# Matrix square root and spectral layer on one core: earlier loads for the inverse transform, a schedule of three rounds in ten, filler matmuls, and a reordered start

## The chip, the cores and the metric

One core of a Trainium2 chip. The metric is device time in microseconds (us) of one execution. The kernel before took 3040.89 us, the median of three runs (3040.22 to 3058.99); lower is better. Engines are called TensorE (PE), VectorE (DVE), ScalarE (ACT), GpSimd (POOL) and SyncE (SP). PEld is TensorE's weight load.

## The reference, cut to what matters

The input x is (32 images, 32 channels, 128, 128) in float32. Each layer normalises x in 16 groups of two channels, transforms it, and adds the result to x.

```python
def _L0_conv_ref(A):                    # layer 0: matrix square root of every 128 x 128 channel
    normA = jnp.sqrt(jnp.sum(A2 * A2, axis=(1, 2)))
    Y = A2 / normA[:, None, None]; Z = I
    for _ in range(5):
        T = 0.5 * (3.0 * I - jnp.matmul(Z, Y)); Y = jnp.matmul(Y, T); Z = jnp.matmul(T, Z)
    return Y * jnp.sqrt(normA)[:, None, None]

def _L1_conv_ref(x, weights1, weights2): # layer 1: mixing of channels on low frequencies
    x_dht = fftn(x).real
    top = einsum('bixy,ioxy->boxy', x_dht[:, :, :32, :32], weights1)
    bot = einsum('bixy,ioxy->boxy', x_dht[:, :, -32:, :32], weights2)
    return ifftn(out_dht).real           # out_dht: zeros, with top and bot put in

x = x + _L0_conv_ref(_gn(x))
x = x + _L1_conv_ref(_gn(x), weights1, weights2)
```

## The kernel before

**Layer 0.** The work unit is a quartet: four channels of an image, 256 in all. prep (line 208) computes an image's statistics and scales: it loads eight tiles xs (two groups each) through ScalarE's DMA queue, in four buffers, three ahead; VectorE takes bn_stats of each; two small matmuls average over partitions; two square roots (root, line 171: a Sqrt on ScalarE and four operations of VectorE) give sc, the scale, and sn, the last factor. After the second root comes off, the offset that ScalarE needs to scale the rows. Only then does made[b] exist, and staged (356) may scale a quartet: POOL makes x from xt, ScalarE makes b. newton (426) then runs the iteration as some twenty steps. In a step TensorE makes four 128x128 products into a PSUM bank (products, 327; a float32 product is two records in the trace), and VectorE or ScalarE takes the bank. POOL adds r = mb + EYE (plus_eye, 313). The last step adds the root to xt (452). settle (458) stores it to the DRAM tensor mid, POOL folds it (halves added and subtracted), and VectorE takes its statistics.

**Layer 1.** After the eighth quartet of an image, forward (476), summed (511) and spectrum (544) compute its low frequencies from the folds. Images come in groups of 20, 7, 3 and 2 (GROUPS). When a group's spectra are there, wide_products, small_products (661) or last_products (740) multiply them with the weights, piece by piece of the frequencies; om holds a result on the chip, and od in DRAM collects it. small_products begins with two memsets on POOL and sixteen or more loads diag<-xs on SP. For the last group, weights() (782) loads the weights into buffers of layer 0 as these come free. Then inverse (887) takes each image: load_products reads ob (for small groups or, which place copies into order as ob), load_input (832) reads mid back as yt in two halves of channels (e = 0, 1; two tiles of 512 KB each). TensorE transforms the rows (pg, copied by ScalarE as gt) and then the columns (py). For each half e and each tile i, ScalarE copies the odd part as d, VectorE adds the even part to yt, and unfold (857) adds or subtracts d, on POOL (in the tail every other tile on VectorE). store (849) writes yt to the output. The pool page (three buffers) serves om, or and d; yt has six buffers, and in the tail some yt take buffers of fold.

**The order of the work.** Every engine and DMA queue works in the order in which the Python code issues instructions; that order is written by hand, with generators. The main loop (1042) runs rounds. In a round it steps each of nine lanes once, each lane being one quartet's newton. A new quartet starts every 3 rounds for images 1 to 18 and every 5 rounds for the others. Between the lanes it steps the other queues once: preps (1070), specs, posts, prods (the products), and backs (the inverse). prods is stepped in two of three rounds, backs in the third, and backs in the next round too when an inverse stands in the middle of a half (holding). Each yield in inverse is the end of such a turn. With the first yield (893), the one after pg (914) and two for each half, an image inside a group takes four turns, 12 rounds. When no quartet is left, tail is true, all these queues are stepped for every lane, and the stores go to ScalarE's DMA queue instead of SP's. From image 20 on, inverse, products and the last quartets run beside each other.

**Queues.** SP's queue carries mid, turn, the weights, od, ob or or, yt and, before the tail, the output. A DMA on it that waits (for a buffer, or for POOL's result) holds everything behind it. ScalarE's queue carries x, xt and xs, in line with ScalarE's own operations.

Of the kernel before, what the change touches and what calls it, by code (L numbers as in the profile page):

```python
# [36 lines left out]
P = 128  # L37
# [51 lines left out]
def conv_preact_kernel(  # L89
# [78 lines left out]
    def bank():  # L168
        return ps8.tile([P, 4, P], F32, tag="ps", name="ps")

    def root(v, n, tag):

        s0 = small.tile([P, n], F32, tag="root_0", name=f"{tag}_s0")
        nc.scalar.activation(s0, v, AF.Sqrt)
        yield
        q = small.tile([P, n], F32, tag="root_1", name=f"{tag}_q")
        nc.vector.reciprocal(q, s0)
        nc.vector.tensor_mul(q, q, v)
        nc.vector.tensor_tensor(q, q, s0, ALU.add)
        s = small.tile([P, n], F32, tag=f"{tag}_s", name=f"{tag}_s", bufs=3 if tag == "a_t" else 2)  # L180
        nc.vector.tensor_scalar_mul(s, q, 0.5)
        return s

    def moments(st, ms, tag):

# [22 lines left out]
    def prep(bs, made):  # L208

        n = len(bs)  # L210
        nc_, ng = n * C, n * G
        first_b = bs[0]
        st = small.tile([P, ng, 6], F32, tag="a_st", name=f"a_st{first_b}", bufs=2)
        tiles = []
        parts = [(b, i) for b in bs for i in range(C // 4)]

        def load(k):
            b, i = parts[k]
            t = stp.tile([P, 2, 2 * P], F32, tag="xs", name=f"xs{b}_{i}")
            src = xs_in[b, :, 2 * i : 2 * i + 2].rearrange("p g h c -> p g (h c)")  # L220
            kept(nc.scalar.dma_start(out=t, in_=src))
            tiles.append(t)

        for k in range(3):
            load(k)
        yield
        for k in range(len(parts)):
            for j in range(2):
                nc.vector.bn_stats(st[:, 2 * k + j, :], tiles[k][:, j, :])
            yield  # L230
            if k + 3 < len(parts):
                load(k + 3)
        ms = small.tile([P, ng], F32, tag="a_ms", name=f"a_ms{first_b}")
        nm, d = yield from moments(st, ms, "a")
        yield from pause
        pq = bank()[:, 0, 0:nc_]
        nc.tensor.matmul(pq, avg_mean, d.rearrange("p g c -> p (g c)"), start=True, stop=True)

        v = small.tile([P, nc_ + ng], F32, tag="a_v", name=f"a_v{first_b}")
        nc.vector.tensor_scalar_mul(v[:, 0:nc_], pq, -512 / (P * P))  # L240
        yield
        vg = small.tile([P, ng], F32, tag="a_vg", name=f"a_vg{first_b}")
        nc.vector.tensor_reduce(
            vg, v[:, 0:nc_].rearrange("p (g c) -> p g c", c=2), AX.X, ALU.add
        )
        nc.vector.tensor_scalar(v[:, nc_:], vg, 0.5, EPS, ALU.mult, ALU.add)
        yield
        s = yield from root(v, nc_ + ng, "a_r")
        iv = small.tile([P, nc_ + ng], F32, tag="a_inv", name=f"a_inv{first_b}")
        nc.vector.reciprocal(iv, s)  # L250
        yield

        sc = small.tile([P, nc_], F32, tag="a_sc", name=f"a_sc{first_b}", bufs=2)
        nc.vector.tensor_scalar_mul(sc, iv[:, 0:nc_], MS / P)
        nn = small.tile([P, ng, 2], F32, tag="a_d", name=f"a_n{first_b}")
        nc.vector.tensor_tensor(
            nn,
            s[:, 0:nc_].rearrange("p (g c) -> p g c", c=2),
            iv[:, nc_:, None].to_broadcast([P, ng, 2]),
            ALU.mult,  # L260
        )
        nn = nn.rearrange("p g c -> p (g c)")
        nc.vector.tensor_scalar_mul(nn, nn, P * (1.5 / (EYE * QF)) ** 2)
        yield
        sn = yield from root(nn, nc_, "a_t")

        off = small.tile([P, ng, 2], F32, tag="a_off", name=f"a_off{first_b}", bufs=2)
        nc.vector.tensor_tensor(
            off,
            sc.rearrange("p (g c) -> p g c", c=2),  # L270
            nm[:, :, None].to_broadcast([P, ng, 2]),
            ALU.mult,
        )
        off = off.rearrange("p g c -> p (g c)")
        for k, b in enumerate(bs):
            g, c = slice(k * G, k * G + G), slice(k * C, k * C + C)
            made[b] = (nm[:, g], sc[:, c], off[:, c], sn[:, c])
        yield


# [145 lines left out]
    def newton(g, sn, xt, m, mb, far, more):  # L426


        q = yield from quartic(m, mb, far, more, False)
        my = four("my", more)  # L430
        y = my[:, :, 0, :]
        nc.scalar.mul(y, products(q, m), 1 / (MS * QF))
        yield from rest
        m = my[:, :, 1, :]
        nc.scalar.mul(m, products(q, y), MS / QF)
        yield from rest
        mb = taken(transposed(m), "mb", more)
# [12 lines left out]
        t = plus(products(w, q), -0.5 * EYE / (1.5 * QF), eye, "t", more)  # L450
        yield from rest
        nc.vector.tensor_tensor(xt, products(t, y), xt, ALU.add)
        yield

    folds = {}
# [88 lines left out]
    def spectrum(b, u):  # L544
# [40 lines left out]
        if i == len(xs):  # L585

            for e, t in enumerate(diags):
                for l4 in range(4):
                    rows = slice(32 * l4, 32 * l4 + 32)
                    copy = nc.scalar.copy if l4 % 2 else nc.vector.tensor_copy  # L590
                    copy(
                        t.rearrange("p (m b l f) -> p m b l f", b=2, l=4, f=4)[rows, :, j, l4, :],
                        spec[rows, 8 * e : 8 * e + 8].rearrange("p k q (h f) -> p (k q h) f", f=4),
                    )
            yield
            return
        kept(
# [142 lines left out]
    def last_products(i):  # L740
# [4 lines left out]
        for kk in range(KK):  # L745
# [25 lines left out]
            if kk % 4 == 3:  # L771
                for f in range(4):
                    queue = nc.scalar if f % 2 else nc.sync
                    kept(
                        queue.dma_start(
                            out=od[i][f, kk - 3 : kk + 1].rearrange("k r x -> r k x"),
                            in_=om[f::4, :, f, :].rearrange("p (k h) o -> p k (h o)", h=2),
                        )
                    )
        yield  # L780

    def weights():
# [104 lines left out]
    def inverse(b):  # L887


        more = where[b][1] < GROUPS[where[b][0]] - 1  # L890
        load_products(b)
        load_input(b, 0)
        yield
        if b not in placed:
            place(b)
            if not tail:
                yield
# [12 lines left out]
        for e in range(2):  # L910
            gts.append(inv.tile([P, 4, P], F32, tag="gt", name=f"gt{b}_{e}", bufs=3))
            nc.scalar.copy(gts[e], pg[e])
        unfold()
        yield
        for e in range(2):
# [16 lines left out]
            for i in range(2):  # L932
# [11 lines left out]
                if not i:  # L944
                    holding.append(b)
                    yield
                    holding.pop()
            if not e:
                load_input(b, 1)
            elif more:  # L950
                load_input(b + 1, 0)
                place(b + 1)
            yield
        if not more:
            unfold()
# [79 lines left out]
            yield  # L1035

    preps.append(prep([0], made))
    coming = [((0, 0), [1])] + [((b - 2, 4 if b < FIRST else 2), [b, b + 1]) for b in range(2, B, 2)]
    fetch(*fetches.pop(0))
    stage()  # L1040
    fetch(*fetches.pop(0))
    while todo or any(lanes) or posts or specs or prods or backs:
# [3 lines left out]
        for i in range(LANES):  # L1046
# [26 lines left out]
                step(specs)  # L1073
            if i == 3 or tail:
                step(posts)
            if i == 0 and rounds % 3 or tail:
                step(prods)
            if i == 0 and (rounds % 3 == 0 or holding) or tail and not (posts or specs):
                step(backs)
        rounds += 1  # L1080

# [68 lines left out]
```

## Time and profile before

| | |
|---|---|
| median of three runs | 3040.89 us |
| the profiled execution | 3037.9 us, its span 3035.8 us |
| granted TensorE clock, mean | 0.983 |
| busy: PE | 2878.3 us (95%), 27076 records |
| busy: PE weight load | 2675.2 us (88%) |
| busy: DVE | 2263.7 us (75%) |
| busy: ACT | 1644.0 us (54%) |
| busy: POOL | 1987.6 us (65%) |
| DMA | 636.39 MB, mean 210 GB/s |

The span is the time from the first to the last instruction. The times in the text below are microseconds from its start. All instructions are recorded at line 83, a helper that keeps them in the order of the program, so groups are told apart by the names of their tiles: ps is a PSUM bank, and out<-in gives the tile written and those read. A row of the timeline is: start, busy time, engine, operation, tiles, forms, count, and in brackets how long the engine had been idle before and what ended that. Rows with SPq or ACTq are DMAs issued by that engine's queue; their duration is the time over which the issues spread, waits between them included. For several instructions in one row, the duration is the sum of busy time on an engine.

### The profile page before, as it was taken

The page shows a single profiled execution, that of the slowest core. Times are in us where ns is not written, and L with a number is a line of the kernel's source. Part 1 is how long each engine was busy: PE and PEld are TensorE (multiplying, and loading weights), DVE is VectorE, ACT ScalarE, POOL GpSimd, SP SyncE. Part 2 cuts the span into 40 slices and gives each one's busy share as a digit, 9 for nine tenths or more (in the row PEclk, how much of TensorE's full clock was granted, in tenths as well). Part 3 has the DMA queues.
Part 4 walks back from the last instruction along what each step waited for, and adds up shares of the span by engine and source line. Part 5 has one row for each costly group of instructions (what it writes and reads, how often), then busy time and mean ns, then how long its engine had stood idle before and what let it go on. Part 6 is the DMA issues. An engine that isn't in the chain of part 4 may idle for free. (4 is left out here: it accounts for less than half of the span.)

```text
span 3035.8 us, 73213 instructions
## 1 busy us (share of the span) xinstructions
PE 2878.3 (95%) x27076; PEld 2675.2 (88%) x27076; DVE 2263.7 (75%) x4261; ACT 1644.0 (54%) x4187; POOL 1987.6 (65%) x2306
## 2 busy tenths in 40 slices
PE   6999999999999999999999999999999999898973
PEld 6899999999999999999999889889888889797863
DVE  6778787878787888778876656877778767776654
ACT  3566565665656665565644445555555555564442
POOL 4577677777777776767765435678777774675542
PEclk9999999999999999999999999999999999999986
DMA  5576676777675768575733567667667677575585
GB/s 173 163 231 206 213 215 214 215 214 222 201 232 189 240 190 247 182 240 185 246 109 105 169 205 233 234 215 254 235 205 258 230 249 241 178 233 179 183 265 187
DMA packets 476658, 636.39 MB, mean 210 GB/s; under 512 B 97040, under 2 KB 257296, under 8 KB 476304
## 3 DMA queue, kind: packets, MB, share of 16 engines
q1 hardware_dynamic: 362400, 422.21, 43.3%
q10 hardware_dynamic: 113904, 209.50, 22.3%
q8 instruction: 217, 3.56, 0.5%
q14 instruction: 137, 1.12, 0.1%
HBM read 402.42 MB, written 229.11 MB: 208 GB/s over the span
## 5 line engine op out<-in xcount | busy, mean ns | idle before, releaser
L83 PE MATMUL ps<-my,q 128*128 128x128 f32 (+1 forms) x4096 | 736.4, 329 | 12.7 <-DVE v L83 9.8
L83 PEld LDWEIGHTS ps<-my,q 128*128 128x128 f32 x4096 | 625.8, 191 | 71.5 <-DVE v L83 11.4
L83 POOL TENSOR_TENSOR w<-w,r 128x512 f32<-128x512 f32 x288 | 366.7, 1275 | 379.2 <-DMA w<-turn 308.7
L83 PE MATMUL ps<-w,v 128*128 128x128 f32 x4096 | 552.5, 278 | 25.1 <-DVE w L83 12.4
L83 ACT ACTIVATE b<-b,a_off,a_sc 128x128 f32<-128x128 f32 x1024 | 469.8, 492 | 173.1 <-issue 47.5
L83 POOL TENSOR_TENSOR fold<-xt 128x256 f32<-128x256 f32 x512 | 363.3, 731 | 285.0 <-DVE xt L83 256.2
L83 PEld LDWEIGHTS ps<-w,v 128*128 128x128 f32 x4096 | 503.2, 193 | 40.0 <-DVE w L83 11.8
L83 ACT ACTIVATE my<-ps 128x512 f32<-128x512 f32 x512 | 306.1, 604 | 351.1 <-PE ps L83 333.7
L83 DVE SCALAR_TENSOR_TENSOR q<-ps,eye 128x512 f32<-128x512 f32 x512 | 350.4, 685 | 180.6 <-PE ps L83 175.8
L83 POOL TENSOR_TENSOR yt<-yt,d 128x512 f32<-128x512 f32 x242 | 304.3, 1280 | 273.1 <-ACT d L83 240.7
L83 ACT ACTIVATE t<-ps 128x256 f32<-128x256 f32 x512 | 191.2, 382 | 356.6 <-PE ps L83 345.7
L83 POOL TENSOR_TENSOR r<-mb,eye 128x512 f32<-128x512 f32 x256 | 326.3, 1275 | 79.1 <-ACT mb L83 79.1
L83 POOL TENSOR_SCALAR x<-xt,a_nm,a_sc 128x128 f32<-128x128 f32 x736 | 321.6, 450 | 21.3 <-DVE a_n L83 18.7
L83 POOL TENSOR_TENSOR r<-b,eye 128x512 f32<-128x512 f32 x256 | 326.5, 1275 | 2.7 <-ACT b L83 2.7
L83 ACT ACTIVATE y<-ps,a_t_s 128x128 f32<-128x128 f32 x1024 | 291.2, 375 | 0.0
L83 PE MATMUL ps<-x,b 128*128 128x128 f32 x2048 | 274.9, 278 | 7.5 <-POOL x L83 5.7
L83 PE MATMUL ps<-x,q 128*128 128x128 f32 x2048 | 274.4, 277 | 4.0 <-DVE q L83 2.2
L83 PE MATMUL ps<-y,t 128*128 128x128 f32 x2048 | 273.8, 277 | 2.3 <-DVE t L83 2.3
L83 PE MATMUL ps<-my,mb 128*128 128x128 f32 x2048 | 273.6, 277 | 0.4 <-DVE q L83 0.4
L83 PE MATMUL ps<-q,t 128*128 128x128 f32 x2048 | 274.1, 277 | 0.0
L83 DVE STREAM_TRANSPOSE turn<-v 128x512 f32<-128x512 f32 x288 | 264.9, 920 | 9.9
L83 PEld LDWEIGHTS ps<-x,b 128*128 128x128 f32 x2048 | 251.3, 193 | 11.0 <-POOL x L83 6.0
(121 smaller groups left out, 4481.1 us busy)
## 6 DMA issues: line engine op xcount, KB each, us to landing
turn<-turn SPq DMA_DIRECT2D x288, 256.0 KB
b<-in_x ACTq DMA_DIRECT2D x256, 256.0 KB
xt<-in_xt ACTq DMA_DIRECT2D x256, 256.0 KB
xs<-in_xs ACTq DMA_DIRECT2D x256, 256.0 KB
mid<-xt SPq DMA_DIRECT2D x256, 256.0 KB
yt<-mid SPq DMA_DIRECT2D x128, 512.0 KB
out<-yt SPq DMA_DIRECT2D x113, 512.0 KB
w<-turn SPq DMA_DIRECT2D x144, 256.0 KB
```

The lines of the kernel that those rows point to most:

```text
L83: return self.tc.keep_in_program_order(issue(*args, **kw))
```

## The change

Five edits:

- **Start.** The first image's prep issues all eight xs loads at once (four tiles from the pool xs, four from early buffers of the tile turn), and the main program steps it once ahead of the loads of the first quartet. The offset off and made[b] come ahead of the second root, whose result sn is a tile made early and filled later; root writes into a tile that it is given.
- **inverse.** An image whose ob is already placed no longer has the first turn (load, yield). The load of the second half of yt stands right behind the copies gt, a turn and a half sooner, with a store ahead of it; another store stands behind the turn in the middle of a half. In the tail, load_products and place of the next image come one image sooner.
- **Rounds.** backs is stepped in rounds 0, 3 and 7 of ten, prods in the other seven.
- **warm.** A new function issues matmuls of 512 columns that nothing reads: five in the first image's prep, two after the last quartet's last product, two after the last spectrum, nine after the last products. They lie on TensorE's queue and take a PSUM bank.
- **Names** of the tiles in root.

```diff
+    def warm(n):
+        ps = bank()
+        for _ in range(n):
+            nc.tensor.matmul(ps, ident, tab[:, 0:512], start=True, stop=True)
...
-    def root(v, n, tag):
+    def root(v, n, s):
...
+        ahead = 3 if first_b else 8
         def load(k):
             b, i = parts[k]
-            t = stp.tile([P, 2, 2 * P], F32, tag="xs", name=f"xs{b}_{i}")
+            if first_b or i < 4:
+                t = stp.tile([P, 2, 2 * P], F32, tag="xs", name=f"xs{b}_{i}")
+            else:
+                t = four("turn", True).rearrange("p (j c) x -> p j (c x)", j=2)
...
-        for k in range(3):
+        for k in range(ahead):
             load(k)
...
-            if k + 3 < len(parts):
-                load(k + 3)
+            if k + ahead < len(parts):
+                load(k + ahead)
...
         nc.tensor.matmul(pq, avg_mean, d.rearrange("p g c -> p (g c)"), start=True, stop=True)
+        if not first_b:
+            warm(5)
...
         nc.vector.tensor_scalar_mul(sc, iv[:, 0:nc_], MS / P)
+        off = small.tile([P, ng, 2], F32, tag="a_off", name=f"a_off{first_b}", bufs=2)
+        nc.vector.tensor_tensor(off, ...)
...
+        sn = small.tile([P, nc_], F32, tag="a_t_s", name=f"a_t_s{first_b}", bufs=3)
+        for k, b in enumerate(bs):
...
+            made[b] = (nm[:, g], sc[:, c], off[:, c], sn[:, c])
+        yield
...
-        sn = yield from root(nn, nc_, "a_t")
...
+        yield from root(nn, nc_, sn)
         yield
...
         nc.vector.tensor_tensor(xt, products(t, y), xt, ALU.add)
+        if not todo and lanes.count(None) == LANES - 1:
+            warm(2)
         yield
...
+            if tail:
+                warm(2)
             yield
             return
...
+        warm(9)
         yield
...
     def inverse(b):
         more = where[b][1] < GROUPS[where[b][0]] - 1
-        load_products(b)
-        load_input(b, 0)
-        yield
         if b not in placed:
+            load_products(b)
+            if tail and more:
+                load_products(b + 1)
+            load_input(b, 0)
+            yield
             place(b)
...
             nc.scalar.copy(gts[e], pg[e])
+        if tail and more:
+            place(b + 1)
+        store()
+        load_input(b, 1)
         unfold()
         yield
...
                     yield
                     holding.pop()
-            if not e:
-                load_input(b, 1)
-            elif more:
+                    store()
+            if e and more:
                 load_input(b + 1, 0)
-                place(b + 1)
+                if b + 1 not in placed:
+                    place(b + 1)
             yield
...
     preps.append(prep([0], made))
+    step(preps)
...
-            if i == 0 and rounds % 3 or tail:
+            turn = rounds % 10 in (0, 3, 7)
+            if i == 0 and not turn or tail:
                 step(prods)
-            if i == 0 and (rounds % 3 == 0 or holding) or tail and not (posts or specs):
+            if i == 0 and (turn or holding) or tail and not (posts or specs):
                 step(backs)
```

More of the change, by code (lines that the diff above doesn't have):

```diff
@@ L169, in bank @@
         return ps8.tile([P, 4, P], F32, tag="ps", name="ps")
-    def root(v, n, tag):
-        s0 = small.tile([P, n], F32, tag="root_0", name=f"{tag}_s0")
+    def warm(n):
[3 more added lines that the diff above has]
+    def root(v, n, s):
+        s0 = small.tile([P, n], F32, tag="root_0", name="root_0")
         nc.scalar.activation(s0, v, AF.Sqrt)
         yield
-        q = small.tile([P, n], F32, tag="root_1", name=f"{tag}_q")
+        q = small.tile([P, n], F32, tag="root_1", name="root_1")
         nc.vector.reciprocal(q, s0)
@@ L179, in root @@
         nc.vector.tensor_tensor(q, q, s0, ALU.add)
-        s = small.tile([P, n], F32, tag=f"{tag}_s", name=f"{tag}_s", bufs=3 if tag == "a_t" else 2)
         nc.vector.tensor_scalar_mul(s, q, 0.5)
-        return s
     def moments(st, ms, tag):
@@ L247, in prep @@
         yield
-        s = yield from root(v, nc_ + ng, "a_r")
+        s = small.tile([P, nc_ + ng], F32, tag="a_r_s", name=f"a_r_s{first_b}", bufs=2)
+        yield from root(v, nc_ + ng, s)
         iv = small.tile([P, nc_ + ng], F32, tag="a_inv", name=f"a_inv{first_b}")
@@ L254, in prep @@
         nc.vector.tensor_scalar_mul(sc, iv[:, 0:nc_], MS / P)
+        off = small.tile([P, ng, 2], F32, tag="a_off", name=f"a_off{first_b}", bufs=2)
+        nc.vector.tensor_tensor(
+            off,
+            sc.rearrange("p (g c) -> p g c", c=2),
+            nm[:, :, None].to_broadcast([P, ng, 2]),
+            ALU.mult,
+        )
+        off = off.rearrange("p g c -> p (g c)")
+        sn = small.tile([P, nc_], F32, tag="a_t_s", name=f"a_t_s{first_b}", bufs=3)
+        for k, b in enumerate(bs):
+            g, c = slice(k * G, k * G + G), slice(k * C, k * C + C)
+            made[b] = (nm[:, g], sc[:, c], off[:, c], sn[:, c])
+        yield
         nn = small.tile([P, ng, 2], F32, tag="a_d", name=f"a_n{first_b}")
@@ L264, in prep @@
         yield
-        sn = yield from root(nn, nc_, "a_t")
[L267 to L277, printed above, removed]
+        yield from root(nn, nc_, sn)
         yield
```

## The prediction, made before the changed kernel was run

> **What bounds the kernel now.** First the page, part 2 (busy tenths in 40 slices of 75.9 us; PEclk is the granted TensorE clock).
>
> ```profile
> PE   6999999999999999999999999999999999898973
> ...
> PEclk9999999999999999999999999999999999999986
> ```
>
> TensorE is full from the second slice to about the 37th, so only the first slice, the last three and dips between can give time. Busy time by stretch (columns: stretch, length, then busy us of PE, PE weight load, DVE, ACT, POOL, then clock, DMA share, GB/s) sizes them:
>
> ```profile
> 1000.00:1500.00 500.00, 494.39 (x4129) 467.06 (x4128) 413.30 (x775) 299.31 (x777) 357.76 (x396) 1.00 0.71 218
> ...
> 2750.00:2800.00 50.00, 37.69 (x397) 33.35 (x396) 30.41 (x49) 22.48 (x54) 32.40 (x36) 0.95 0.55 174
> ...
> 2940.00:2960.00 20.00, 2.62 (x23) 1.23 (x24) 5.68 (x15) 2.62 (x3) 5.80 (x6) 0.54 0.85 288
> ...
> 2980.00:3000.00 20.00, 3.39 (x16) 2.38 (x16) 7.71 (x11) 3.12 (x8) 5.48 (x4) 0.57 0.67 207
> ```
>
> In a full stretch PE is busy 494 of 500 us. The hole at 2750 has 12 us without PE; the stretches from 2940 to 3036 have 31.8 us of PE work in 96 us, at a clock of 0.54 to 0.77. Three timelines (start, busy us, engine, operation, idle before and what ended it) show why. The start:
>
> ```profile
> 1.66 8.88 ACTq L83 DMA_DIRECT2D xs<-in_xs  x8
> ...
> 7.46 2.71 DVE L83 BATCH_NORM_STATS2 a_st<-xs 128x6 f32<-128x256 f32 x8 [5.74 <-DMA xs<-in_xs]
> ...
> 22.12 0.49 ACT L83 ACTIVATE b<-b,a_off,a_sc 128x128 f32<-128x128 f32 x1 [1.62 <-DVE a_off L83]
> ...
> 22.71 2.05 PE L83 MATMUL ps<-x,b 128*128 128x128 f32 x8 [5.67 <-POOL x L83]
> ...
> 29.06 0.75 DVE L83 BATCH_NORM_STATS2 a_st<-xs 128x6 f32<-128x256 f32 x2 [3.57 <-DMA xs<-in_xs]
> ```
>
> ScalarE's queue issues the first image's eight loads over 8.9 us, because four buffers hold them; statistics end at 14.55 (13.14 + 1.41), TensorE's first real product is at 22.71, when the first scaled row of b is ready, and at 29.06 VectorE stands 3.57 us on the second image's load. The hole:
>
> ```profile
> 2799.80 1.29 DVE L83 TENSOR_TENSOR yt<-ps,yt 128x512 f32<-128x512 f32 x2 [11.55 <-DMA yt<-mid]
> ...
> 2801.74 3.69 PE L83 MATMUL ps<-my,q 128*128 128x256 f32 x8 [9.83 <-DVE v L83]
> ```
>
> VectorE waits 11.55 us for the second half of image 26's rows (yt<-mid); v stands behind it, and TensorE behind v. That load was issued only at 2791.59, behind sixteen diag<-xs loads (2777.74, 9.70 us on SP). The tail:
>
> ```profile
> 2941.16 5.83 SPq L83 DMA_DIRECT2D yt<-mid  x2
> ...
> 2950.03 1.29 DVE L83 TENSOR_TENSOR yt<-ps,yt 128x512 f32<-128x512 f32 x2 [11.72 <-DMA yt<-mid]
> ...
> 2951.24 0.68 DVE L83 TENSOR_TENSOR xt<-ps,xt 128x512 f32<-128x512 f32 x1
> ...
> 2952.97 27.77 SPq L83 DMA_DIRECT2D yt<-mid  x4
> ...
> 2980.85 9.06 SPq L83 DMA_DIRECT2D od<-om  x6
> ...
> 2987.93 0.69 DVE L83 COPY om<-ps 128x512 f32<-128x512 f32 x1 [12.94 <-DMA od<-om]
> ```
>
> VectorE waits 11.72 us for yt of image 28; the last xt stands behind it, though its product was finished at 2939.5. Later SP stands up to 27.77 us in yt loads that wait for buffers, the od stores stand behind them, and the om copies wait 12.94 us for the page that these stores read. Then the last two images:
>
> ```profile
> 3004.12 2.08 PE L83 MATMUL ps<-tab,ob 64*128 64x128 f32 x16 [12.18 <-ACT ob L83]
> ...
> 3018.94 0.59 ACT L83 COPY gt<-ps 128x512 f32<-128x512 f32 x1 [3.05 <-PE ps L83]
> ```
>
> **What the Trainium skill says.** "TensorE: Matmul & The Clock Gate", Part 1 (The HAM clock gate): the clock halves after an idle window of about 3.4 us and comes back after one busy window. The trace agrees: eight records of w,v take 2.08 us at 30.46 and 1.06 at 2887.72. The same part: VectorE and ScalarE are strict FIFO. The trace agrees: xt at 2951.24 stood behind yt. "Trainium Kernel Development and Optimization", Key Constraints: SP's and ACT's DMAs share the same 16 engines. From 2920 to 2940 they are 0.96 busy at 308 GB/s, so a load that is issued sooner there isn't sooner by as much. "SBUF — State Buffer", Who interferes with whom: a VectorE operation with two SBUF inputs waits for a GpSimd one that reads SBUF. The trace agrees: a 128x96 a_r_q product took 1.29 us at 2198.70 beside a yt pair on POOL, against 0.21 for 128x48 at 18.73.
>
> **The change, part by part**, against the execution's own span of 3035.8 (its time 3037.9; median of the runs 3040.89, so 5.1 is added to the span's sum).
>
> *Start.* All eight xs loads go out ahead of b and xt. The table and xs are 2.39 MB; 1.85 MB came from about 2.7 to 9.3 (280 GB/s), so the last lands at about 11, plus 0.7 for its statistics: 11.6 against 14.55, -3.0. The chain to a_sc keeps its 5.1 us: 19.86 becomes 16.9. The offset stands right behind it instead of behind a square root and four operations (21.87): another -2.0. So the first product could start at 17.7 instead of 22.71. But five warm products stand ahead of it in PE's queue, from 14.0. One is 512 columns, as much as one group of four 128-column products (eight records, 0.89 us a group in the tail, 1.7 to 2.1 cold): two to four cold and the rest warm are 6.0 to 7.7 us, ending 20.0 to 21.7. The first group then takes 1.06 instead of 2.05 and ends at 21.1 to 22.8 against 24.76: -2.0 to -3.7. Second image's statistics come a few rounds later, as the rest of the root is now stepped first: VectorE's stand before 29.73 (w had its inputs at 27.3) can go, 0 to -2.4. I take **-4.5**, bounds -2 and -6. After that PE is full, so it lasts.
>
> *Rows sooner, three rounds in ten.* Operations are the same in number; stores and loads on SP change place. An image now takes three turns instead of four: 10 rounds against 12. I counted rounds in the order of the programs: the last inverse of group 0 ends in round 820 instead of 858, of image 26 in 960 instead of 972, and small_products of the third group starts in 962 in both. So the sixteen diag<-xs loads no longer stand ahead of image 26's rows: -9.8 of PE wait, -1.8 for a cold group (3.69 against 1.89), +1.5 for a diag<-xs wait that stays and now has less beside it: **-10**. Against it, denser inverse work: on POOL 46 of the r additions stood right behind yt sums before, 40 now, but of x and fold right behind two of them 5 become 21. I take this at nothing, since PE has at most 6 us in 100 free here and others' work covers it; if that cover is gone, up to +10; if fewer r waits (56 us on VectorE in all) win, -6.
>
> *Tail, up to the first om.* Image 28 is three rounds ahead, and its second half is loaded ahead of mb, v and w weights: issued at about 2930 instead of 2941. The SP queue was given about 7.25 MB from 2921 to 2941 at some 320 GB/s, so I let it land near 2939 to 2940, where VectorE needs it at 2936: a stand of 2 to 3 us instead of 11.72. The stall goes to POOL: yt27_24's pair (2.5 us) now stands ahead of the last lane's r (+2.2), and yt28_24's pair, done by VectorE before, ahead of the last fold. Adding POOL's queue from 2922 in its new order (1.27 an operation, folds 1.4) ends the fold at 2946.4, against 2955.72: **-9.3**. From there to the first om copy are 13.1 us, 7.3 of them PE at half clock; the two pairs of warm products can halve a part: **-2** (bounds -3.5 and +1.3, if a cold pair, 3.4 us, holds up the first product).
>
> *The om wait.* By the addresses of the tiles yt30_24 takes yt28_24's buffer, and om3_8 still takes om3_0's page. That yt28 store stands on ACT right behind the first od pair now, not behind the second: from om to its landing 8.0 us instead of 11.1; then SP issues one yt load instead of two ahead of od, 0.5 MB less. om3_0 to om3_8 is 13.4 us instead of 19.1: **-5.7** (bounds -2 and -8). From om3_8 to the or loads I take 0: om3_12 now stands behind one more unfolding, +1, but 1 MB of yt29 ahead of od is gone, up to -3.
>
> *Last two images.* Nine warm products (8 us, up to 11) lie in the 14 us of od's way to memory and back: at nothing, +2 if they start late. With them -1 for each first group and pg, **-2**. ob31 is copied before image 30's yt, so pg31 is hidden; gt31 still stands on ACT behind two stores of image 30: 3018.94 becomes 3015.7, **-3**.
>
> Tail: -9.3 - 2 - 5.7 - 2 - 3 = **-22**. Sum -4.5 - 10 - 22 = -36.5: span 2999.3, about **3004** on the scale of the median.
>
> **Rivals.** B, the hole only moves: the PE wait of 2750 is replaced by another (21 x or fold additions behind two pairs; denser ACT and VectorE work). For it: PE has small gaps from 1900 to 2700 wherever yt runs; against: what stood there was one SP queue, which is empty of diag loads now. Mid 0 to +2: 3014 to 3016. C, the tail stays gated: the 16 DMA engines are full at 2920 to 2950, yt28_24 lands at 2945 or the buffer of yt30 again holds od. For it: share 0.96 and 0.85; against: the v, w and mb weights (1.5 MB) now stand behind it. Tail only -8 to -10: 3016 to 3018. D, the other side: not faster, because POOL becomes the bound of the near stage. Place: r behind two unfoldings, w on VectorE behind r, TensorE behind w, as at 2203.01, where PE stood 3.78 us. Price: one more pair, 2.5 us, in each of the 27 images of groups 0 and 1: +67, so 3071. It decides from 36.5/27 = 1.35 us an image. Against: POOL is at 65%, and r's directly behind pairs got fewer. E, the tail gains more: od lands as soon as it is issued and the clock stays whole, -10 more: 2992. That the change does nothing is excluded for the start and image 26 by the order of the queues.
>
> **How the numbers follow.** Forecast 0.52 (own range 2993 to 3012), B 0.20, C 0.16, D 0.06, E 0.06. One per cent is 30.4 us, 3010.5, about what a measurement of this kernel can tell from no change. Below it are E and most of the forecast's own range (0.46 of 0.52), and 0.04 of B and C: 0.56 faster. Slower by over 1% is the upper part of D, 0.05; within, 0.39. The range 2990 to 3026 takes in forecast, B, C and half of E, with the bound of denser work on B.
>
> **What would show it.** Right: first x,b product near 21 and eight records in about 1.1 us; no yt<-mid wait above 4 us on VectorE; image 26 finished before diag<-xs; last xt near 2942 less the 14 saved before; the om wait below 9 us; PEclk above 0.8 in the last slices. Wrong: PE waits behind r or x of over 3 us from 1900 to 2700 that sum to more than before (steps B, D); a long yt wait on SP ahead of od (C); a first product that waits for warm ones beyond 23.

## The result, and the profile after

The changed kernel took 3009.16 us, the median of four runs (3001.22 to 3015.01), against 3045.48 before on the same chip: ratio 0.9872, 95% interval 0.9829 to 0.9915. Measured again later (six runs) it was 3006.2 against 3043.57: 0.9878, 0.9854 to 0.9902. The forecast was 3004, range 2990 to 3026. The profiled execution took 3011.95 us with a span of 3010.2 (before 3037.9 and 3035.8). The spans differ by 25.6 us, the medians by 36 to 37: the profiled execution of before lies 3 to 11 us below the medians that before had in the later measurements (3041.16 to 3048.71).

The page, part 2, after (busy tenths of PE and granted clock, 40 slices):

```profile
PE   8899999999999999999999999999999999999995
...
PEclk9999999999999999999999999999999999999997
```

The last six slices read 999995 instead of 898973, the first 8 instead of 6, and the clock ends in 97 instead of 86. Fillers count as busy here: PE is busy for 2899.0 us in all instead of 2878.3, and fillers are 22.1 us of it. But the kernel without any fillers (below) also ends in 999994. Busy time by stretch, columns as before (stretch, length, busy us of PE, PE weight load, DVE, ACT, POOL, then clock, DMA share, GB/s):

```profile
1000.00:1500.00 500.00, 492.73 (x4114) 465.51 (x4113) 407.46 (x773) 298.81 (x774) 357.68 (x396) 1.00 0.70 217
2750.00:2800.00 50.00, 48.37 (x533) 43.91 (x532) 37.71 (x63) 25.20 (x63) 36.02 (x43) 1.00 0.54 185
2940.00:2960.00 20.00, 17.43 (x227) 11.32 (x229) 7.66 (x25) 5.30 (x11) 4.13 (x5) 0.77 0.84 317
2980.00:3000.00 20.00, 9.87 (x96) 7.39 (x96) 16.44 (x22) 8.27 (x20) 7.92 (x6) 0.67 0.71 274
```

The full stretch of the middle is unchanged (494.39 before). The hole at 2750 is closed: 48.37 us of PE in 50 instead of 37.69. In the tail the stretches have moved forward: 2940 to 2960 now holds the first of the last products, which began at 2966 before; 6.0 us of its 17.43 are fillers. The timeline, the start:

```profile
8.32 2.78 DVE L83 BATCH_NORM_STATS2 a_st<-turn 128x6 f32<-128x256 f32 x8
...
13.40 6.33 PE L83 MATMUL ps<-tab,ident 128*128 128x512 f32 x10
...
16.68 0.49 ACT L83 ACTIVATE b<-b,a_off,a_sc 128x128 f32<-128x128 f32 x1 [2.16 <-DVE a_off L83]
...
19.57 1.05 PE L83 MATMUL ps<-x,b 128*128 128x128 f32 x8
```

Statistics end at 11.10 instead of 14.55; the first real product comes at 19.57 instead of 22.71, at the full clock, directly behind the fillers (13.40, 6.33 us). Its first row of b was ready at 17.17. The tail:

```profile
2927.52 1.20 SPq L83 DMA_DIRECT2D yt<-mid  x2
...
2936.03 2.54 DVE L83 TENSOR_TENSOR yt<-ps,yt 128x512 f32<-128x512 f32 x4 [6.24 <-DMA yt<-mid]
...
2938.49 0.68 DVE L83 SCALAR_TENSOR_TENSOR t<-ps,eye 128x512 f32<-128x512 f32 x1
...
2939.32 2.04 PE L83 MATMUL ps<-y,t 128*128 128x128 f32 x8 [7.97 <-DVE t L83]
...
2941.40 0.69 DVE L83 TENSOR_TENSOR xt<-ps,xt 128x512 f32<-128x512 f32 x1 [2.23 <-PE ps L83]
...
2950.58 13.01 SPq L83 DMA_DIRECT2D yt<-mid  x4
...
2967.65 0.69 DVE L83 COPY om<-ps 128x512 f32<-128x512 f32 x1 [5.65 <-DMA od<-om]
```

The stand of VectorE on yt of image 28 is still there, 6.24 us instead of 11.72. It now stands ahead of the last quartet's t as well; the last product waits for that t, runs at half clock (2.04 us; 1.06 at full clock), and only then comes the last xt. SP's stand in the yt loads is 13.01 instead of 27.77, and the om copies wait 5.65 instead of 12.94. The last two images:

```profile
2981.04 1.16 PE L83 MATMUL ps<-tab,ob 64*128 64x128 f32 x16 [3.08 <-ACT ob L83]
...
2991.10 1.09 ACT L83 COPY gt<-ps 128x512 f32<-128x512 f32 x2
...
2991.39 3.44 DVE L83 TENSOR_TENSOR yt<-yt,d 128x512 f32<-128x512 f32 x2
```

gt31 comes 10.1 us behind the start of pg30 (2981.04) instead of 14.8. The last line is longer than its counterparts before: two VectorE additions of yt take 3.44 us beside two of POOL; at this place in the last two images they took 2.37 and 2.84.

**Where the time went, from events.** The 256 additions of xt come in the same order in all kernels, so their ends date the stages. (The first row is the time from the span's start, the others are stretches, in us; worked out from the traces.)

| stage | before | after | after, second profile |
|---|---|---|---|
| 160th xt (last of the first group) | 1668.7 | 1668.7 | 1665.6 |
| 160th to 248th | 1188.8 | 1180.1 | 1177.6 |
| 248th to the end of the last fold | 98.2 | 95.4 | 95.9 |
| to the first om copy | 12.5 | 12.2 | 11.3 |
| to the third page's om copy | 19.7 | 11.3 | 11.4 |
| to pg30 | 16.2 | 13.4 | 13.1 |
| to the end | 31.7 | 29.2 | 30.0 |

From the last fold on there are 14 us, 8.4 of them in the om wait; about 10 lie between quartets 160 and 248. In a single trace the first row wanders: ten traces with the same instructions up to there have it between 1658.8 and 1668.7 (mean 1663.9), and the three with the start of before at 1664.5, 1668.7 and 1671.5. Only medians can judge the start.

### The profile page after: what moved, and what is told of

The parts are those of the page before. It is cut to its first block, busy times and chain, and to the rows that moved or that the text cites. A ratio compares the mean times of both kernels' runs of the same rounds, so it can differ in the third digit from the quotient of the medians.

```text
span 3010.2 us, 73284 instructions
## 1 busy us (share of the span) xinstructions
PE 2899.0 (96%) x27112; PEld 2683.7 (89%) x27112; DVE 2266.7 (75%) x4259; ACT 1642.3 (55%) x4187; POOL 1990.6 (66%) x2308
## 5 line engine op out<-in xcount | busy, mean ns | idle before, releaser
L83 PEld LDWEIGHTS ps<-w,v 128*128 128x128 f32 x4096 | 501.5, 192 | 36.9 <-POOL w L83 11.4
L83 POOL TENSOR_SCALAR x<-xt,a_nm,a_sc 128x128 f32<-128x128 f32 x736 | 323.2, 455 | 15.6 <-DVE a_sc L83 15.2
L83 PEld LDWEIGHTS ps<-y,t 128*128 128x128 f32 x2048 | 254.6, 194 | 12.5 <-issue 8.1
```

The lines of the kernel that those rows point to most:

```text
L83: return self.tc.keep_in_program_order(issue(*args, **kw))
```

## The experiments

Theory: the gain is one of order. Loads and stores on SP's queue stand ahead of what used to hold them; the clock and the fillers matter little. Rivals: the clock made the tail (fillers); the pace, not the order of the loads, closed the hole; denser inverse work costs what it brings.

Medians, and ratios to before on the same chip (the changed kernel in its second measurement):

| kernel | median us | ratio, 95% interval |
|---|---|---|
| start alone | 3035.9 | 0.998, 0.9968 to 0.9991 |
| inverse and rounds alone | 3008.0 | 0.9886, 0.9862 to 0.991 |
| rows sooner alone | 3023.8 | 0.9936, 0.992 to 0.9951 |
| changed | 3006.2 | 0.9878, 0.9854 to 0.9902 |
| changed, no fillers in the tail | 3009.3 | 0.9891, 0.9867 to 0.9915 |
| changed, no fillers at the start | 3007.9 | 0.987, 0.9843 to 0.9897 |
| changed, every third round | 3013.1 | 0.9907, 0.9886 to 0.9929 |
| changed, every fourth round | 3007.0 | 0.9884, 0.9858 to 0.991 |
| changed, rows late | 3011.4 | 0.9893, 0.9869 to 0.9918 |
| changed, image 28's rows sooner | 3003.2 | 0.9868, 0.9844 to 0.9892 |
| two paces | 3001.9 | 0.9864, 0.9847 to 0.988 |
| two paces, od first | 2998.7 | 0.9847, 0.9828 to 0.9866 |

The kernels ran on four chips, each beside the kernel before; between kernels of different chips the ratios are the fairer comparison.

**One part alone.** First the start: before with the edits of prep (its five fillers too), root and the main program's extra step.

> Only the edits of the start (eight loads at once, offset ahead of the second root, five filler products); inverse, rounds and tail as before. The prediction's step: -4.5 us, and it lasts because PE is full afterwards, so 0.9985 of the time before. Rival, read from the profile after: the first product is 3.1 us earlier and the eighth quartet ends 6.5 us earlier, but the sixteenth only 1.9 and the 144th 0.1 us, because the first quartets of the far images wait for their own chain (the turned w through DRAM) and not for PE's beginning. Then 0.999 to 1.000, and the trace shows the lead of the first quartets gone by 1500 us.

Ratio 0.998: the medians differ by 5.3 us, so the prediction's -4.5 stands. The rival was read from one trace; that nothing is left of the start is excluded, a gain of only 3 us is not (the interval ends at 0.9991). The lead of 1.9 us at the sixteenth quartet was the chance of that execution: this kernel's trace has 7.4 us there. Then inverse and rounds alone, without any fillers:

```diff
-        load_products(b)
-        load_input(b, 0)
-        yield
         if b not in placed:
+            load_products(b)
...
             nc.scalar.copy(gts[e], pg[e])
+        if tail and more:
+            place(b + 1)
+        store()
+        load_input(b, 1)
...
-            if i == 0 and rounds % 3 or tail:
+            turn = rounds % 10 in (0, 3, 7)
+            if i == 0 and not turn or tail:
```

> Only the edits of inverse and the rounds (three in ten); start as before, no filler products anywhere. My theory: this is most of the change: hole at 2750 about -10, the wait for yt of image 28, the om wait and the last two images -16 to -18 together, so -26 to -28, ratio 0.991. Rival 1: the tail is won by the clock that the fillers keep up, then only the hole, -10 to -14, ratio 0.996. Rival 2: as the fillers cost a PE queue place too (a cold pair held up the first last product by 1.5 us), this alone is as good as the whole change, -33 to -36, ratio 0.988 or 0.989.

33 us of the 36 to 37. It is more than my -26 to -28, and the rival "fillers useless" met the ratio. With the start, and without the tail's fillers:

```diff
-        if not todo and lanes.count(None) == LANES - 1:
-            warm(2)
...
-            if tail:
-                warm(2)
...
-        warm(9)
```

> The changed kernel without the three filler places of the tail (two after the last quartet, two after the last spectrum, nine after the last products); the five of the start stay. My theory, from the sum of the prediction: fillers of the tail are worth 2 (fold to om) and 2 (last two images), less what the cold pair costs: +2 to +5 us against the changed kernel, ratio to before 0.989. Rival 1 (clock is what made the tail): +10 or more, ratio 0.991 or above; the trace then shows the fold, pg and py products of the last images at 2 to 3.5 us instead of 1.1. Rival 2 (fillers useless): 0 or a gain, ratio 0.987 or below.

3 us slower than the changed kernel by medians, 4 by ratios, inside the intervals of both. The clock rival, 10 us or more, is at the edge of this interval, and the traces speak against it: from the last fold to the end are 68.9 us here and 65.7 in the kernel without any fillers, against 66.0 and 65.9 with them. The last fold's products take 1.97 us here instead of 1.09, and from the fold to the first om copy are 12.6 us, against 12.2 and 11.3 with fillers. The pair of fillers behind the last spectrum ran at half clock in the first profile of the changed kernel (3.62 us, 1.88 in the second), and the first of the last products started 2.1 us behind the start of the diag copies there, 0.9 us in the kernel before: in that execution it was held up by some 1.2 us.

**Order or pace.** Three kernels. The changed one at every fourth round:

```diff
-            turn = rounds % 10 in (0, 3, 7)
+            turn = rounds % 4 == 0
```

> The changed kernel with inverse stepped in every fourth round: an image takes 12 rounds, as before, in three turns; image 26 ends in round 972, as before, so after small_products of the third group has started (962), but its second half of rows is loaded at its first turn, round 956, ahead of the diag loads. Theory A (order on SP's queue made the hole): the hole stays closed all the same, no yt<-mid wait of more than 3 us near 2760 to 2800, and image 28 ends in round 1028 instead of 1027: within 4 us of the changed kernel. Theory B (the pace of three in ten, by which image 26 is through before the third group starts, is what closed the hole): the hole comes back, +8 to +12.

Theory A holds for the hole. No yt<-mid wait is left there, though image 26 ends behind the start of the third group; what is left is one wait of TensorE for the diag loads themselves:

```profile
2783.76 1.06 PE L83 MATMUL ps<-plain,diag 128*12 128x32 f32 x64 [3.95 <-DMA diag<-xs]
```

Then before with nothing but the load put forward (and the stores that free its buffers):

```diff
             nc.scalar.copy(gts[e], pg[e])
+        store()
+        load_input(b, 1)
         unfold()
...
-            if not e:
-                load_input(b, 1)
-            elif more:
+                    store()
+            if e and more:
```

> The kernel before with one part of the change alone: the load of yt's second half stands behind the gt copies, with the two stores that free its buffers; four turns, every third round, start and tail as before. Image 26 still ends in round 972, but its load now stands five places ahead of the third group's first diag loads. Theory A (the order on SP's queue made the hole at 2750): the yt<-mid wait of 11.5 us goes, and with it -8 to -10 us; the wait for yt of image 28 shrinks little, because that load still stands behind the v and w weights (place 1271 of SP's queue, 1264 in the changed kernel): 0 to -3; in all -8 to -13, ratio 0.996 to 0.997. Theory B (the pace closed the hole, the order of the load is nothing): 0 to -2, ratio 0.999 to 1.0.

Its stretch at the hole, against 37.69 us of PE before:

```profile
2750.00:2800.00 50.00, 46.02 (x464) 40.78 (x463) 39.24 (x61) 25.32 (x62) 35.11 (x38) 1.00 0.57 187
```

Theory A again, and more than I expected: 19 us by medians. In its trace the 248th xt is only 3.5 us ahead of before, and the 160th already was by 4.2, where the instructions are still the same; from the first to the third page's om copy are 15.2 us instead of 19.7 (SP stands 21.90 us in the yt loads ahead of od instead of 27.77). The trace accounts for 10.6 us (its span), 4.2 of them chance, not for all 19. Then the other side, the changed kernel with the load put back to the end of the first half:

```diff
-        load_input(b, 1)
         unfold()
         yield
...
+            if not e:
+                load_input(b, 1)
             if e and more:
```

> The changed kernel with the load of the second half of yt put back to the end of the first half (a turn and a half later); the pace and everything else as changed. My theory: the hole at 2750 stays closed, since at the new pace image 26's load still stands ahead of the third group's diag loads; the tail loses: the load of yt28's second half goes out some 6 to 8 us later, behind the v and w weights, so that VectorE's stand of 6.2 us becomes 10 to 12 and the last xt comes 4 to 6 us later: +4 to +6 us against the changed kernel, ratio about 0.989. Rival: the 16 DMA engines are full there (share 1.05), so the load lands when it lands, and the time is within 2 us of the changed kernel.

```profile
2931.18 1.15 SPq L83 DMA_DIRECT2D yt<-mid  x2
...
2939.46 2.51 DVE L83 TENSOR_TENSOR yt<-ps,yt 128x512 f32<-128x512 f32 x4 [15.34 <-DMA yt<-mid]
```

The hole stays closed, as expected: at three rounds in ten even the late load is ahead of the diag loads. In the tail VectorE stands 15.34 us, more than I had expected, and the 248th to the 256th xt take 102.5 us instead of 93.8. Of these 8.7 us the median shows 5, inside the uncertainty. The rival, that the load lands when it lands, is refuted by the trace: counted from the 248th xt the load goes out 8.9 us later than in the second profile of the changed kernel, and lands 8.6 us later.

Side by side, from events (us):

| kernel | 160th to 248th xt | 240th to 244th | TensorE idle in these | TensorE's wait for diag<-xs near 2460 |
|---|---|---|---|---|
| before | 1188.8 | 69.9 | 14.1 | 3.38 |
| start alone | 1196.2 | 70.6 | 14.6 | 3.37 |
| rows sooner alone | 1189.6 | 59.7 | 4.0 | 5.99 |
| changed, every fourth round | 1190.8 | 62.3 | 4.5 | 6.31 |
| changed, rows late | 1176.7 | 55.5 | 2.0 | none |
| changed | 1180.1 | 55.1 | 1.6 | none |

The hole is the 240th to the 244th quartet. The order of the load takes 10 us of idle out of it, and the new pace closes it without that order. But only with the new pace is the whole stretch from 160 to 248 shorter in these traces. With the load put forward at 12 rounds an image, TensorE's wait for the second group's diag loads has grown from 3.4 to about 6 us; the rest is not placed, and before and start alone, with the same instructions here, already differ by 7.4 us.

**Is density free?** Every third round, the pace before, with the three turns of the changed kernel:

```diff
-            turn = rounds % 10 in (0, 3, 7)
+            turn = rounds % 3 == 0
```

> The changed kernel with inverse stepped in every third round as before (an image takes 9 rounds, not 10; last inverse of the first group ends in round 801 instead of 820, image 26 in 954 instead of 960, before it was 972); the products are stepped in two rounds of three again. My theory: what matters for the hole is only that image 26 ends before small_products of the third group starts (round 962), so the hole stays closed, and the rest is within 4 us of the changed kernel: ratio 0.986 to 0.989. Rival (step D of the prediction: density costs on POOL): 10 per cent denser inverse work makes PE wait more between 1700 and 2450 (PE idle there grew by 8 us from before to after), so +5 to +10 against the changed kernel.

7 us slower than the changed kernel by medians, 9 by ratios; the intervals overlap in part. TensorE's gaps of over 1 us from 1700 to 2740 sum to 33.6 us, against 28.7 in the changed kernel and 27.6 before. That sum alone proves nothing: over all traces it lies between 24.5 and 33.7 us at three rounds in ten, and between 27.6 and 35.7 in the three traces with the density of before. But the three longest gaps, 6.05, 4.83 and 3.77 us, follow dense work on POOL. The second of them:

```profile
2363.17 2.50 POOL L83 TENSOR_TENSOR yt<-yt,d 128x512 f32<-128x512 f32 x2
...
2363.70 7.00 DVE L83 TENSOR_TENSOR b_inv<-b_r 128x1 f32<-128x1 f32 x1
...
2365.62 1.27 POOL L83 TENSOR_TENSOR r<-mb,eye 128x512 f32<-128x512 f32 x1
...
2366.84 1.41 POOL L83 TENSOR_TENSOR fold<-xt 128x256 f32<-128x256 f32 x2
2368.21 2.48 POOL L83 TENSOR_TENSOR yt<-yt,d 128x512 f32<-128x512 f32 x2
2370.63 0.68 DVE L83 SCALAR_TENSOR_TENSOR w<-ps,r 128x512 f32<-128x512 f32 x1
...
2371.45 1.83 PE L83 MATMUL ps<-w,v 128*128 128x128 f32 x7 [4.83 <-DVE w L83]
```

POOL works without a gap from 2361.94 to 2370.7. In that time VectorE's product b_inv, a 128x1 tile from two SBUF inputs that mostly takes 0.16 to 0.22 us, is 7.00 us under way; w stands behind it, and TensorE stands 4.83 us for w. The 6.05 us have the same form (a 128x64 product of root, mostly 0.22 us, took 6.01). So what shows here is not the way of rival D, r standing behind yt on POOL, but VectorE kept off while POOL runs. The Trainium skill, "SBUF — State Buffer", Who interferes with whom, has it: a VectorE instruction with two SBUF inputs contends with a GpSimd one that reads SBUF. The trace agrees, and here the product is under way through four POOL groups in a row. Such products are not new: the longest took 4.34 us in the kernel before and 4.12 in the changed one. That this density costs time is likely by the medians; it is not shown.

**The fillers of the start.**

```diff
-        if not first_b:
-            warm(5)
```

> The changed kernel without the five filler products of the start. In the trace of the changed kernel the first row of b is ready at about 17.2 but the first product starts at 19.57, behind the fillers, and its group is warm (1.05 us) and ends at 20.62; by 24 the clock is cold again. My theory: without the fillers the first group starts at 17.3 to 17.7, takes 2.05 cold and ends at 19.4 to 19.8, so the fillers cost the first group about 1 us and give back about as much in the two or three groups behind it: the eighth quartet ends within 2 us of the changed kernel's (132.8), the time within 3 us, ratio 0.987 to 0.989. Rival (the prediction's reading that a warm start is worth having): the cold groups add up, 4 to 6 us later at the eighth quartet, ratio 0.9895.

```profile
17.20 2.05 PE L83 MATMUL ps<-x,b 128*128 128x128 f32 x8 [3.68 <-POOL x L83]
...
28.71 1.06 PE L83 MATMUL ps<-w,v 128*128 128x128 f32 x8
```

The first group starts at 17.20, takes 2.05 us cold, and ends at 19.25 instead of 20.62. The seventh group behind it, w,v, starts at 28.71 instead of 29.46, and the eighth quartet ends at 132.6 instead of 132.8. The fillers of the start bring nothing that shows: in the changed kernel they held back the first group by 2.4 us (17.2 to 19.57), made it 1.0 us shorter, and at 23.97 a group took 1.92 us again.

**Past the change.** Image 28's second half loaded with its first:

```diff
                 load_input(b + 1, 0)
+                if b + 1 == B - 4:
+                    load_input(b + 1, 1)
```

> The changed kernel with the second half of image 28's rows loaded together with its first half, some 12 us sooner, ahead of eight weight loads (2 MB). My theory: the stand of VectorE on yt<-mid (6.2 us in the changed kernel, 7.6 in two others) goes, the last xt comes 5 to 7 us sooner, and POOL's yt pairs end ahead of the last fold: -4 to -7 us against the changed kernel. Rival (the tail is bound by what DMA still has to move: about 7 MB of weights): the weights land as much later and the first last products wait for them, 0 to -2 us.

The stand is gone, and the 248th to the 256th xt take 86.7 us instead of 93.8. But the gain is handed on to the next in line. POOL:

```profile
2930.22 7.42 POOL L83 TENSOR_TENSOR yt<-yt,d 128x512 f32<-128x512 f32 x6
...
2937.58 1.42 POOL L83 TENSOR_TENSOR fold<-xt 128x256 f32<-128x256 f32 x2
```

Six yt additions now stand directly ahead of the last fold. From the last xt to the end of the fold are 4.3 us instead of 2.1, and the third page's om copy, still held by od<-om, comes 13.7 us behind the first instead of 11.4. 7 us sooner at xt are 3.5 at the end (from the 248th xt: 158.2 instead of 161.7), and 3 by medians. The fourth-round kernel had shown a better way: there image 28's second half has its turn behind the last quartet, and the last xt stands behind no such wait. Two paces join that with the denser middle:

```diff
-            turn = rounds % 10 in (0, 3, 7)
+            turn = rounds % 4 == 0 if rounds > 961 else rounds % 10 in (0, 3, 7)
```

> The changed kernel with two paces: three rounds in ten up to round 961 (image 26 ends in 960), every fourth round after it, so that image 28's second half (its turn in round 1028) falls behind the last quartet instead of between its last products. In the traces the changed pace was 13 us ahead of before at quartet 248 (mean of five kernels) against 8 us with every fourth round throughout; from there to the end the fourth-round kernel took 151 us, the changed one 161.6. My theory: both gains add, 3006 - 10 = 2996 to 2999 us, ratio 0.984 to 0.986. Rival (the lead at 248 and the tail's time trade against each other, since work moved out of one stands in the other): within 3 us of the changed kernel, ratio 0.987 or 0.988.

4.3 us below the changed kernel by medians and by ratios, less than the 7 to 10 expected; the intervals overlap. The tail kept its gain (248th xt to the end 152.7 us against 161.7), the middle is that of the changed kernel. Last, image 30's rows off the head of the last products:

```diff
-        for e in range(2):
-            load_input(B - GROUPS[i], e)
         for kk in range(KK):
```

> The kernel with two paces, and image 30's rows are no longer loaded ahead of the last products but in image 30's inverse, behind its or loads: the od stores then stand behind no yt load that waits 12 to 14 us for its buffers. My theory: the wait of the third om copies for od<-om (4.3 to 5 us on ScalarE, 5.7 to 6.4 on VectorE) goes, and with it 4 to 5 us of the tail, less up to 1 us for the yt wait of image 30: ratio 0.0013 below the kernel with two paces. Rival: the rows of image 30 then come late (2 MB behind the or loads, some 6 us), VectorE waits for yt<-mid there, and nothing is gained, -1 to +3 us.

```profile
2958.77 0.68 DVE L83 COPY om<-ps 128x512 f32<-128x512 f32 x1
...
2960.34 0.61 ACT L83 COPY om<-ps 128x512 f32<-128x512 f32 x1
...
2981.47 2.60 DVE L83 TENSOR_TENSOR yt<-ps,yt 128x512 f32<-128x512 f32 x4 [1.02 <-DMA yt<-mid]
```

The om copies no longer wait for od<-om (5.65 us in the two-pace kernel), and the third page's comes 5.7 us behind the first instead of 11.4; one wait for od<-om stays, 3.41 us of ScalarE ahead of a copy of d. In exchange VectorE waits 1.02 us for image 30's rows, and from the third page's copy to pg30 are 15.5 us instead of 13.5. It is 3 us below the two-pace kernel by medians and 44 below before. The interval, 0.9828 to 0.9866, touches that of the changed kernel (0.9854 to 0.9902), so this version beats before clearly and the changed kernel probably.

## Why the prediction was right

The sum, -36.5, met medians that differ by 36.3 and 37.4. That is in part luck. From the 248th xt to the end the two profiles are 16.8 and 16.5 us shorter, where the tail was put at 22, and what makes up for it is not placed; within the tail, terms were off in opposite directions.

- **Start, -4.5: right,** -5.3 alone. Statistics ended at 11.10 (said: 11.6), the fillers took 6.33 us (6.0 to 7.7), the first group ended at 20.62 (21.1 to 22.8). The stand on the second image's load fell from 3.57 us to 0.66 and 0.31. The fillers are no part of the gain: without them the kernel is as fast within the intervals, and by the prediction's own figures the first group, from 17.7 and cold, would have ended at 19.8.
- **Rows and pace, -10: right.** From quartet 160 to 248 the two profiles show -8.7 and -11.2; at the hole itself -14.8 and -14.5, and some of that was lost elsewhere or by chance. The reason given, sixteen diag loads ahead of image 26's rows, is shown by the two kernels above in which image 26 ends as late as before and its load alone stands ahead. It named the pace as the cause; the sooner load closes most of the hole too, but with it alone the stretch as a whole is no shorter in the traces.
- **Density at nothing: not contradicted at three in ten** (gaps of 28.7 us against 27.6, inside what traces of one pace scatter). At one in three a price is likely.
- **Tail up to the first om, -9.3 - 2: mis-sized.** This is the step that failed. "A stand of 2 to 3 us" was 6.24 and 6.67 in the two profiles (7.71 with inverse and rounds alone), over the 4 us that the prediction had named as its limit, and the fold came 2.8 and 2.3 us sooner within this stage, not 9.3. The landing was right: the load took 8.5 us from its issue (2927.52 to 2936.03), 9 to 10 were said. The issue was wrong: counted from the 248th xt it stands at 78.8 us instead of 83.6, so 4.8 us sooner, not 11 (2930 instead of 2941). VectorE came to it where it had come before, at 81.1 (before 80.8), so it needed the load 2.3 us after the issue (2936.03 - 6.24 - 2927.52), not 6. Most of that gain was lost again on the way to the last xt, which came 1.2 us behind the landing before and comes 5.4 us behind it now, because t and the last product stand between. So it ends 93.4 us behind the 248th instead of 94.4, at 2942.1, where the prediction's sign was 2942 less 14. Rival C named this outcome for the tail's first stage, but not its way: that a load issued sooner into full DMA engines (share 1.07 from 2920 to 2940) isn't sooner by as much is not what the kernel with rows late shows. The -2 for the clock was -0.3 and -1.2.
- **The om wait, -5.7: too small.** From the first to the third page's copy it was -8.4 and -8.3. The order named is the reason: SP's stand ahead of od fell to 13.01 us, and in the kernel with od first the om copies do not wait at all.
- **Last stretch.** From the third page's om copy to pg30 -2.8 and -3.1, where nothing was said. gt31 was 4.8 us sooner behind pg30, 3 were said, but from pg30 to the end only 2.5 and 1.7 were won (-5 expected, with the clock): from 2984.68 to 3005 VectorE has no gap over 0.03 us, so it is the bound there. The two additions at 2991.39 took 3.44 us beside POOL's; two at 2969.45, with POOL idle, took 1.28.
- **Rivals.** B and D did not come at this pace: no gap of TensorE near the hole is over 2 us. Of E the whole clock did not come: pg30 took 1.16 us in one profile and 2.08 in the other. Its 2992 should be 2994 by its own sum; nothing hangs on it. The Trainium skill, "TensorE: Matmul & The Clock Gate", Part 1 (The HAM clock gate), gives an idle window of about 3.4 us, and the traces agree: the nine fillers ended 3.08 us ahead of pg30 in the first and 4.50 us in the second.

What stays open: single traces account for 25.6 to 31 us of the 36 to 37, and for 10.6 of the 19 of the rows alone; the rest is not placed. What delays the second group's diag loads when only the load is put forward was not followed. A kernel with the new pace and image 26's rows still behind the diag loads, which would show that the hole comes back, was not tried.

## What to carry over

When a wait for a transfer ends a stall, look at what stands ahead of it on the issuing queue, and move the issue, before changing any work; one load put forward, with the stores that free its buffers, gave half of this change by medians. When the stall goes, follow what comes next: here from VectorE to POOL's queue, then to SP's stores, then to VectorE's plain throughput. Read a gain at the place where it should arise and over the whole stretch: a hole can close without the stretch getting shorter. And look for the edge of a pace by trying one step denser.

## What the runs showed of the hardware

- A VectorE product that mostly takes 0.16 to 0.22 us was under way for 7.00 us while POOL worked without a gap.
- 1 MB issued into nearly full DMA engines (share 1.00 to 1.07) landed 8.5 and 8.3 us after its issue, and an issue 8.9 us later landed 8.6 us later.
- Leads of a few us that are read from one trace prove nothing here: ten traces with the same instructions up to quartet 160 reached it up to 10 us apart.
- Fillers for TensorE's clock: leaving out those of the tail cost 3 us by medians, inside the intervals; leaving out those of the start cost nothing that shows.
